# A two-layer decoder on one core: another order of the layers, and one more set of narrow heads under way

## The chip, the core and the metric

The kernel runs on one NeuronCore of a Trainium2 chip. Its engines work side by side, each through a queue of its own: TensorE (PE in the profile, PEld for its weight loads) multiplies, VectorE (DVE) and ScalarE (ACT) work element by element, GpSimd (POOL) does the same more slowly, and SyncE (SP) issues transfers between the device's memory (HBM) and the on-chip memory (SBUF). Matrix products land in PSUM[...]. The metric is the device time of one execution in microseconds; lower is better.

## What is computed

`x` is 16 sequences of 128 positions of 256 numbers. Six layers follow one another, each as `x = layernorm(x + f(x))`:

```
0  wide attention   16 heads of 64, causal: softmax(q k' / 8) v, then W_O
1  ensemble         8 experts, each relu(x P_in') P_out', weighted by a gate per token
                    gate[b,s,e] = sum_k ctx[b,k,s] * (itok[b,k,s] == e)
2  routed           2 shared experts + 16 routed ones, top 2 of a softmax over 16 logits;
                    every expert computed, h = silu(x wg) * (x wu) * comb
3  narrow attention 16 heads of 16, band of +-8 positions
4  cross attention  16 heads of 16, keys and values from ctx
5  dense experts    8 experts of gelu(x w1 + b1) w2 + b2, summed, one scale per token
```

All of it is in float32. No sequence looks at another one, so the 16 sequences are independent; within a sequence each layer needs the one before.

## The kernel before

**Tiling.** The sequences are cut into four groups of four (`GB = 4`, `T = 512` tokens). A group's activations stay on chip as `x` (tokens on partitions) and, rebuilt after each layer by `tail`, as the transposed `xT`. A pair (layer, group), such as (3, 2), is the unit of work in what follows.

**Pieces and streams.** Each layer is a Python generator. It issues a handful of instructions and then yields an estimate of their TensorE time in microseconds, or `UNTIL` with a moment before which the next piece had better not be issued. A `Weaver` decides whose piece comes next. It keeps a clock `now`, which is the sum of the yielded estimates, and it takes a piece from a *main* stream and a *side* stream by their shares: each piece adds its estimate, divided by that stream's figure in the pair `us`, to the stream's share, and the stream with the smaller share goes next among those whose `UNTIL` has come. Short streams (the transposes, routing and gates of `tail`) go ahead of both. The engines then run their queues in the order so woven, moved about a little by the framework's scheduler; nothing of the weaving exists at run time. All real waiting is by semaphores, and PSUM and SBUF buffers come from small rotating pools.

**Main and side.** The attentions (layers 0, 3 and 4) are the main stream, one group after another. The dense layers (1, 2 and 5) are the side stream `dense`, one chain (lines 880 to 883). A layer of a group may begin when the tail of the layer before has been issued (`run`, line 847):

```python
        yield lambda: written[g] == number - 1
```

Before, the main stream's (0, 0) goes alone, then seven stretches each weave one group's attention with the side chain, and the rest of `dense` goes alone at the end.

**Layer 1 to layer 2.** After (1, g) its tail transposes `x`, then `route` (lines 670 to 726) makes 16 small matmuls (L675), some twenty short DVE instructions in a chain (softmax, best of 16 twice, weights, ending in `r_o`, L715), a transpose of `r_o` on TensorE (line 720) and a transfer to HBM. Only then may (2, g) begin, with the matmuls that read `ws`.

**Dense layers.** `accumulate` (line 578) keeps one chunk ahead: it issues the products `psH` of chunk i + 1 (L289), whose result ACT (Gelu, L813, layer 5) or DVE (L650, layer 1) turns into `hT`, and then the eight passes `psM` of chunk i that read `hT` (L589).

**Wide attention**, `attention0` (line 343): 16 units of two pairs of heads and one sequence. Each goes through scores `psS` (L384), softmax, transposes of the weights `e` (L51), weighing with `v` (L426) and output (L393).

**Narrow attention**, `attention16` (line 447), serves layers 3 and 4: 8 units of one sequence and half of the heads. A unit's scores take two matmuls of 64 rows (L464, halves k = 0 and k = 1) into the only `psS` buffer. `softmax` (line 306) takes a minimum with the mask (layer 3 alone), row maxima on DVE, eight Exp instructions with their sums on ACT (L325), reciprocals on DVE and the scaling of `e` on POOL (L331). Then come eight transposes of `e` on TensorE (L51), two copies to `eT` on ACT (L340), eight passes with `v` (L476), and `hz` and `zT`. The loop of lines 500 to 522 is a software pipeline: in round n it issues the scores of unit n, the transposes of unit n - 1, the output of n - 3 and the weighing of n - 2. It holds the transposes back by 14 us of the weaver's clock after the scores. The pool of `e` has three buffers, that of `eT` four (two for each unit).

Of the kernel before, what the change touches and what calls it, by code (L numbers as in the profile page):

```python
# [27 lines left out]
def kernel(ctx: ExitStack, tc: tile.TileContext, a: dict, out: bass.AP):  # L28
# [15 lines left out]
    def bank(tag):  # L44
        return ps.tile([P, T], F32, tag=tag, name=f"ps{tag}")
# [7 lines left out]
    def together(first, *steps):  # L53

        for step in steps:
            tc.add_manual_dep(
                first.ins, step.ins.name,
                mybir.DependencyInfo(mybir.DependencyClass.Sync, mybir.DependencyReason.DATA),
                reason="together",
            )  # L60
# [172 lines left out]
    weaver = Weaver()  # L233
# [72 lines left out]
    def softmax(s, seen):  # L306

        n = 2 * s.shape[2]
        if seen is not None:
            sm = p2.tile([P, n, P], F32, tag="s", name="sm")  # L310
            nc.vector.tensor_tensor(
                sm.rearrange("p (s h) k -> p s h k", s=2), s,
                seen.unsqueeze(1).unsqueeze(1).to_broadcast([P, 2, n // 2, P]), ALU.min,
            )
        nmax = sp.tile([P, n], F32, tag="nmax", name="nmax")
        if seen is not None:
            nc.vector.tensor_reduce(nmax, sm, AX.X, ALU.max, negate=True)  # L317
        else:
            nc.vector.tensor_reduce(  # L319
                nmax.rearrange("p (s h) -> p s h", s=2), s, AX.X, ALU.max, negate=True  # L320
            )
        e = p3.tile([P, n, P], F32, tag="p", name="e")
        total = sp.tile([P, n], F32, tag="total", name="total")
        for h in range(n):
            nc.scalar.activation(  # L325
                e[:, h, :], sm[:, h, :] if seen is not None else s[:, h // (n // 2), h % (n // 2), :],
                AF.Exp, bias=nmax[:, h:h + 1], accum_out=total[:, h:h + 1],
            )
        inv = sp.tile([P, n], F32, tag="inv", name="inv")
        nc.vector.reciprocal(inv, total)  # L330
        nc.gpsimd.tensor_tensor(e, e, inv.unsqueeze(2).to_broadcast([P, n, P]), ALU.mult)  # L331
        return e

    def weights_T(e):

        pt = bank("O").rearrange("p (h q) -> p h q", h=4)
        for h in range(4):
            transpose(pt[:, h, :], e[:, h, :])
        eT = p4.tile([P, 4, P], F32, tag="pt", name="eT")
        return eT, nc.scalar.copy(eT, pt)  # L340
# [106 lines left out]
    def attention16(x, qT, kT, v, wo, bo, seen):  # L447
        norm = Norm(x)
        norm.bias(bo)

        def scores(b, c):

            at = slice(b * P, (b + 1) * P)

            kb = p2.tile([P, 4, P], F32, tag="kb", name="kb")
            nc.gpsimd.tensor_tensor(  # L456
                kb, kT[:, c, at].unsqueeze(1).to_broadcast([P, 4, P]),
                hm4.unsqueeze(2).to_broadcast([P, 4, P]), ALU.mult,
            )
            yield UNTIL, weaver.now + 2.0  # L460
            s = ps.tile([P, 2, T], F32, tag="S", name="psS", bufs=1)
            for k in range(2):
                rows = slice(64 * k, 64 * k + 64)
                mm(  # L464
                    s[:, k, :], lhsT=qT[rows, c, at], rhs=kb[rows].rearrange("p h k -> p (h k)"),
                    start=True, stop=True,
                )
            return softmax(s.rearrange("p s (h k) -> p s h k", h=4), seen)

        def weigh(b, c, eT):  # L470


            pz = bank("O")[:, :D].rearrange("p (k q) -> p k q", k=2)
            for r in range(4):
                rows = slice(32 * r, 32 * r + 32)
                step = mm(  # L476
                    pz[rows], lhsT=v[:, b, c * P + 32 * r:c * P + 32 * r + 32],
                    rhs=eT[r // 2][0][:, 2 * (r % 2):2 * (r % 2) + 2, :],
                    start=True, stop=True,
                )  # L480
                if r == 0:
                    together(step, eT[1][1])
            if c == 0:
                zT[b] = p3.tile([P, 2, P], F32, tag="z", name="zT16")
            half_z = p2.tile([P, P], F32, tag="hz", name="hz")
            nc.scalar.activation(half_z, pz[:, 0, :], AF.Copy, scale=even[:, 0:1])
            nc.vector.scalar_tensor_tensor(
                out=zT[b][:, c, :], in0=pz[:, 1, :], scalar=even[:, 1:2], in1=half_z,
                op0=ALU.mult, op1=ALU.add,
            )  # L490

        def output(b):
            po = bank("H")[:, :D]
            for k in range(KC):
                mm(po, lhsT=zT[b][:, k, :], rhs=wo[:, k, :], start=k == 0, stop=k == KC - 1)  # L495
            norm.add(b, po)

        units = [(b, c) for b in range(GB) for c in range(2)]
        e, eT, zT, at = {}, {}, {}, {}
        for n in range(len(units) + 4):  # L500
            if n < 8:
                e[n] = yield from scores(*units[n])
                at["e", n] = weaver.now + 14.0
                yield 1.06
            m = n - 1
            if m in e:
                yield UNTIL, at["e", m]
                got = e.pop(m)
                eT[m] = [weights_T(got[:, 4 * k:4 * k + 4, :]) for k in range(2)]
                at["t", m] = weaver.now + 3.5  # L510
                yield 1.0
            m = n - 3
            if ("z", m) in at and units[m][1] == 1:
                yield UNTIL, at["z", m]
                output(units[m][0])
                yield 0.86
            m = n - 2
            if m in eT:
                yield UNTIL, at["t", m]
                weigh(*units[m], eT.pop(m))  # L520
                at["z", m] = weaver.now + 3.0
                yield 0.63
        norm.done()
# [321 lines left out]
    def run(number, g):  # L845

        yield lambda: written[g] == number - 1
        x, xT = xs[g], xTs[g]
        if number == 0:
            yield from attention0(x, xT, g)  # L850
        elif number == 1:
            yield from ensemble0(x, xT, g)
        elif number == 2:
            yield from experts0(x, xT, extra[g])
        elif number == 3:
            yield from attention1(x, xT)
        elif number == 4:
            yield from cross1(x, xT, g)
        else:
            yield from experts1(x, xT, extra[g])  # L860
            nc.sync.dma_start(
                out=out[g * GB:(g + 1) * GB].rearrange("b p d -> p b d"), in_=x
            )
            return
        weaver.short.append(Stream(tail(number, g)))

    def chain(*layers):
        for layer in layers:
            yield from run(*layer)

    def sum_biases():
        pb = bank("H")[:, :D]
        mm(pb, lhsT=ones[0:8, :], rhs=b2, start=True, stop=True)
        nc.vector.tensor_copy(b2sum, pb)
        yield 0.5
# [2 lines left out]
    b2sum = cp.tile([P, D], F32, tag="b2sum", name="b2sum")  # L878
    weaver.short += [Stream(tail(-1, g)) for g in range(NG)]
    dense = Stream(chain(  # L880
        (1, 0), (2, 0), (1, 1), (2, 1), (1, 2), (2, 2), (1, 3), (2, 3),
        (5, 0), (5, 1), (5, 2), (5, 3),
    ))
    weaver.weave(Stream(chain((0, 0))))
    weaver.short.append(Stream(sum_biases()))
    weaver.weave(Stream(chain((0, 1))), dense, (81.0, 110.0))
    weaver.weave(Stream(chain((0, 2))), dense, (81.0, 106.0))
    weaver.weave(Stream(chain((0, 3))), dense, (81.0, 106.0))
    weaver.weave(Stream(chain((3, 0), (4, 0))), dense, (68.0, 110.0))
    weaver.weave(Stream(chain((3, 1), (4, 1))), dense, (68.0, 106.0))  # L890
    weaver.weave(Stream(chain((3, 2), (4, 2))), dense, (68.0, 106.0))
    weaver.weave(Stream(chain((3, 3), (4, 3))), dense, (68.0, 110.0))
    weaver.weave(dense)


# [67 lines left out]
```

## Time and profile before

| | |
|---|---|
| median of the runs | 1867.82 us (1865.88 to 1871.24, three runs) |
| the profiled execution | 1863.81 us, its span 1862.1 us |
| matmul instructions on TensorE | 7794, busy 1805.6 us, 97% of the span |
| ScalarE | busy 750.1 us, 40% |
| VectorE | busy 648.7 us, 35% |
| GpSimd | busy 363.0 us, 19% |
| HBM traffic | 129.04 MB read, 71 GB/s over the span |

A float32 matmul appears as two passes in the trace and a transpose as one. Passes overlap in the pipeline, so a pass of 128x512 lasts about 0.6 us in the table of groups, while the next one starts 0.43 us after it; sums of TensorE work are made with such start-to-start times. The windows further down give the busy time of each engine in a stretch, the granted TensorE clock (PEclk) and the traffic.

### The profile page before, as it was taken

The numbers are of one execution on the slowest core, as the hardware profiler recorded it, in microseconds if no ns is written. First come the engines' busy times: TensorE is split into PE (matmuls) and PEld (weight loads), VectorE is DVE, ScalarE is ACT, GpSimd is POOL, SyncE is SP. The second block draws the span as 40 slices with busy tenths as digits, with TensorE's granted clock in tenths as the row PEclk, the third lists the DMA queues.
The fourth block names the chain that finished last, engine by engine and source line by source line (L and its number), as shares of the span: only waits on it lengthen the run. The fifth ranks groups of instructions, "written<-read, shape, count | busy, mean of one in ns | idle before, by whom it ended". The sixth has DMA issues, their size and how long they took to land.

```text
span 1862.1 us, 21229 instructions
## 1 busy us (share of the span) xinstructions
PE 1805.6 (97%) x7794; PEld 1111.5 (60%) x7794; DVE 648.7 (35%) x1359; ACT 750.1 (40%) x2229; POOL 363.0 (19%) x297
## 2 busy tenths in 40 slices
PE   6999999999999999999899999899999999999998
PEld 3656666566666656656455665465565655556665
DVE  3453334434333525343425444333223222312101
ACT  2541222342312333241452423527748468475221
POOL 4210001121101112122332213223122122221000
PEclk9999999999999999999899999999999999999999
DMA  6021123122221132122123121121111111111220
GB/s 233 24 86 57 57 74 102 58 85 74 99 89 37 44 120 101 63 71 66 41 79 108 63 91 34 58 93 66 46 63 57 46 68 46 57 46 68 80 76 26
DMA packets 67272, 132.72 MB, mean 71 GB/s; under 512 B 6600, under 2 KB 34304, under 8 KB 67168
## 3 DMA queue, kind: packets, MB, share of 16 engines
q1 hardware_dynamic: 66240, 129.20, 20.5%
q0 software_dynamic: 928, 2.17, 0.4%
q8 instruction: 62, 1.02, 0.2%
q14 instruction: 42, 0.34, 0.1%
HBM read 129.04 MB, written 2.29 MB: 71 GB/s over the span
## 4 chain that ended last, share of the span: by engine, by line
PE 81%; issue 7%; ACT 5%; DVE 5%; DMA 1%; POOL 1%; SPq 0%; POOLq 0%; DVEq 0%; ACTq 0%
PE psH L289 34%; PE psM L589 23%; PE psH L298 4%; PE psO L51 4%; PE psS L464 3%; PE psH L393 3%; ACT e L325 2%; PE psS L384 2%; PE psO L426 2%; PE psO L476 2%; PE psH L495 1%; PE psH L51 1%; DMA wquad<-in_L_attn_W_Q 1%; ACT L325 1%; DVE x L281 1%
## 5 line engine op out<-in xcount | busy, mean ns | idle before, releaser
L589 PE MATMUL psM<-we,hT 128*128 128x256 f32 x2048 | 496.2, 383 | 3.1 <-ACT hT L813 3.1
L289 PE MATMUL psH<-xT,we 128*128 128x512 f32 x1024 | 488.3, 598 | 1.3 <-DVE hT L650 1.3
L589 PEld LDWEIGHTS psM<-we,hT 128*128 128x128 f32 x2048 | 380.7, 190 | 153.1 <-issue 95.1
L331 POOL TENSOR_TENSOR e<-e,inv 128x512 f32<-128x512 f32 (+1 forms) x128 | 188.2, 1471 | 792.6 <-DVE inv L330 728.2
L289 PEld LDWEIGHTS psH<-xT,we 128*128 128x128 f32 x1024 | 187.4, 190 | 159.9 <-issue 142.0
L325 ACT ACTIVATE e<-sm,nmax 128x128 f32<-128x128 f32 x512 | 198.5, 389 | 152.9 <-DVE nmax L317 152.5
L340 ACT COPY eT<-psO 128x512 f32<-128x512 f32 x192 | 106.0, 586 | 207.2 <-PE psO L51 206.7
L650 DVE SCALAR_TENSOR_TENSOR hT<-psH,gt 128x512 f32<-128x512 f32 x128 | 88.1, 689 | 214.1 <-PE psH L289 214.1
L813 ACT ACTIVATE hT<-psH,b 128x512 f32<-128x512 f32 x128 | 86.9, 687 | 177.1 <-PE psH L289 176.5
L289 PE MATMUL psH<-xT,wquad 128*128 128x512 f32 x256 | 117.7, 603 | 1.3 <-DVE qT L357 0.8
L51 PEld LDWEIGHTS psO<-ident,e 128*128 128x128 f32 x768 | 88.4, 143 | 49.4 <-issue 32.1
L51 PE MATMUL psO<-ident,e 128*128 128x128 f32 x768 | 111.0, 281 | 5.0 <-POOL e L331 4.9
L289 PE MATMUL psH<-xT,wr 128*128 128x512 f32 x256 | 115.8, 594 | 0.0
L456 POOL TENSOR_TENSOR kb<-kT,hm 128x512 f32<-128x512 f32 x64 | 66.9, 1046 | 189.4 <-PE psS L464 128.7
L330 DVE RECIPROCAL inv<-total 128x4 f32<-128x4 f32 (+1 forms) x128 | 23.9, 187 | 216.6 <-ACT e L325 214.0
L325 ACT ACTIVATE e<-psS,nmax 128x128 f32<-128x128 f32 x256 | 90.1, 379 | 21.3 <-DVE nmax L319 20.9
L325 ACT ACTIVATION_READ_ACCUMULATOR e<-sm,nmax 128x1 f32 x512 | 95.8, 187 | 0.0
L464 PE MATMUL psS<-kb,qT 64*128 64x512 f32 x256 | 84.5, 646 | 7.0 <-ACT e L325 6.7
L279 POOL TENSOR_TENSOR rstd<-ve,mhalf 128x4 f32<-128x4 f32 x24 | 24.3, 1012 | 310.0 <-DVE ve L277 309.4
L317 DVE TENSOR_REDUCE nmax<-sm 128x4 f32<-128x512 f32 (+1 forms) x96 | 82.8, 863 | 2.7
L289 PEld LDWEIGHTS psH<-xT,wquad 128*128 128x128 f32 x256 | 47.2, 191 | 58.3 <-issue 50.2
L289 PEld LDWEIGHTS psH<-xT,wr 128*128 128x128 f32 x256 | 48.0, 190 | 49.5 <-issue 46.3
(155 smaller groups left out, 1802.9 us busy)
## 6 DMA issues: line engine op xcount, KB each, us to landing
we<-in_L_ffn_w SPq DMA_DIRECT2D x64, 512.0 KB
we<-in_L_xattn_proj_in SPq DMA_DIRECT2D x32, 512.0 KB
we<-in_L_xattn_proj_out SPq DMA_DIRECT2D x32, 512.0 KB
gt<-gatesd SPq DMA_DIRECT2D x32, 256.0 KB
cw<-combd SPq DMA_DIRECT2D x64, 128.0 KB
wquad<-in_L_attn_W_Q SPq DMA_DIRECT2D x16, 256.0 KB
wquad<-in_L_attn_W_K SPq DMA_DIRECT2D x16, 256.0 KB
wquad<-in_L_attn_W_V SPq DMA_DIRECT2D x16, 256.0 KB
```

The source lines that it names most:

```text
L51: return nc.tensor.transpose(out_, in_, ident[:n, :n])
L289: mm(pt, lhsT=w[:, c, cols], rhs=xT[:, c, :], start=c == 0, stop=c == KC - 1)
L298: mm(pv[:, i, :], lhsT=xT[:, c, (b + i) * P:(b + i + 1) * P], rhs=w[:, c, :], start=c == 0, stop=c == k - 1,)
L317: nc.vector.tensor_reduce(nmax, sm, AX.X, ALU.max, negate=True)
L325: nc.scalar.activation(e[:, h, :], sm[:, h, :] if seen is not None else s[:, h // (n // 2), h % (n // 2), :], AF.Exp, bias=nmax[:, h:h + 1 ...
L331: nc.gpsimd.tensor_tensor(e, e, inv.unsqueeze(2).to_broadcast([P, n, P]), ALU.mult)
L340: return eT, nc.scalar.copy(eT, pt)
L456: nc.gpsimd.tensor_tensor(kb, kT[:, c, at].unsqueeze(1).to_broadcast([P, 4, P]), hm4.unsqueeze(2).to_broadcast([P, 4, P]), ALU.mult,)
L464: mm(s[:, k, :], lhsT=qT[rows, c, at], rhs=kb[rows].rearrange("p h k -> p (h k)"), start=True, stop=True,)
L589: step = mm(acc[b], lhsT=held[:, b * P:(b + 1) * P], rhs=down(i), start=i == 0 and b % 2 == 0, stop=i == n - 1, skip_group_check=True,)
L650: nc.vector.scalar_tensor_tensor(out=hT, in0=ph, scalar=0.0, in1=gates[e], op0=ALU.max, op1=ALU.mult)
L813: nc.scalar.activation(hT, ph, AF.Gelu, bias=b1[:, i:i + 1])
```

## The change

Two things are altered. The pipeline of `attention16` gets one more stage between the scores of a unit and its transposes: in round n it now transposes unit n - 2, weighs n - 3 and outputs n - 4, and the hold-back is 16 us instead of 14. And the two streams are ordered anew: the first two wide attentions go alone; the side chain takes layer 1 of two groups, then layer 2 of the same two groups; the main stream runs in three stretches of two groups each. The figures that set the shares change from 81 : 110 or 81 : 106 to 81 : 150, and from 68 : 110 or 68 : 106 to 68 : 150 for the narrow layers.

```diff
-        for n in range(len(units) + 4):
+        for n in range(len(units) + 5):
             if n < 8:
                 e[n] = yield from scores(*units[n])
-                at["e", n] = weaver.now + 14.0
+                at["e", n] = weaver.now + 16.0
                 yield 1.06
-            m = n - 1
+            m = n - 2
             if m in e:
...
-            m = n - 3
+            m = n - 4
             if ("z", m) in at and units[m][1] == 1:
...
-            m = n - 2
+            m = n - 3
             if m in eT:
...
-        (1, 0), (2, 0), (1, 1), (2, 1), (1, 2), (2, 2), (1, 3), (2, 3),
+        (1, 0), (1, 1), (2, 0), (2, 1), (1, 2), (1, 3), (2, 2), (2, 3),
         (5, 0), (5, 1), (5, 2), (5, 3),
     ))
-    weaver.weave(Stream(chain((0, 0))))
+    weaver.weave(Stream(chain((0, 0), (0, 1))))
     weaver.short.append(Stream(sum_biases()))
-    weaver.weave(Stream(chain((0, 1))), dense, (81.0, 110.0))
-    weaver.weave(Stream(chain((0, 2))), dense, (81.0, 106.0))
-    weaver.weave(Stream(chain((0, 3))), dense, (81.0, 106.0))
-    weaver.weave(Stream(chain((3, 0), (4, 0))), dense, (68.0, 110.0))
-    weaver.weave(Stream(chain((3, 1), (4, 1))), dense, (68.0, 106.0))
-    weaver.weave(Stream(chain((3, 2), (4, 2))), dense, (68.0, 106.0))
-    weaver.weave(Stream(chain((3, 3), (4, 3))), dense, (68.0, 110.0))
+    weaver.weave(Stream(chain((0, 2), (0, 3))), dense, (81.0, 150.0))
+    weaver.weave(Stream(chain((3, 0), (4, 0), (3, 1), (4, 1))), dense, (68.0, 150.0))
+    weaver.weave(Stream(chain((3, 2), (4, 2), (3, 3), (4, 3))), dense, (68.0, 150.0))
     weaver.weave(dense)
```

No instruction of the arithmetic is added or taken away, and none changes its shape. The built program holds the same 4393 matmuls and the same 420 transfers on SyncE, in another order; of the loads of ACT's function tables, which are placed where the order of functions asks for one, there are 102 where there were 109.

## The prediction, made before the change was run

> **What bounds the kernel now.** I read the page first, then windows cut where TensorE's idle time changes character, then the order of time in the worst of them.
>
> ```profile
> PE 1805.6 (97%) x7794; PEld 1111.5 (60%) x7794; DVE 648.7 (35%) x1359; ACT 750.1 (40%) x2229; POOL 363.0 (19%) x297
> PEclk9999999999999999999899999999999999999999
> PE 81%; issue 7%; ACT 5%; DVE 5%; DMA 1%; POOL 1%; SPq 0%; POOLq 0%; DVEq 0%; ACTq 0%
> ```
>
> TensorE is busy 97% of the span. The matmuls stay the same, so only TensorE's waits, its slow clock and the seams between its instructions can change. The windows say where those lie (busy time and instructions by engine, clock, DMA):
>
> ```profile
> 24.00:125.00 101.00, 96.77 (x533) 59.34 (x532) 52.72 (x100) 46.26 (x170) 23.22 (x20) 1.00 0.23 79
> 125.00:896.00 771.00, 767.45 (x3427) 481.85 (x3425) 307.26 (x622) 230.24 (x753) 117.54 (x98) 1.00 0.22 74
> 896.00:922.00 26.00, 18.37 (x87) 9.31 (x88) 14.01 (x40) 14.69 (x61) 9.08 (x7) 0.80 0.12 33
> 922.00:1150.00 228.00, 226.53 (x932) 135.40 (x931) 87.53 (x168) 82.09 (x292) 57.93 (x41) 1.00 0.23 75
> 1150.00:1180.00 30.00, 23.03 (x111) 12.77 (x109) 20.12 (x57) 15.71 (x62) 11.79 (x8) 0.89 0.09 28
> 1180.00:1660.00 480.00, 471.66 (x1941) 280.15 (x1940) 137.70 (x287) 292.50 (x750) 115.30 (x81) 1.00 0.18 62
> ```
>
> Two short windows, 896 to 922 and 1150 to 1180, are bad: TensorE idles 7.6 and 7.0 us and its clock falls to 0.80 and 0.89. The timeline of TensorE in the first (start, us, instructions, idle before):
>
> ```profile
> 907.30 1.30 PE L464 MATMUL psS<-kb,qT 64*128 64x512 f32 x4 [2.65 <-ACT e L325]
> 909.51 1.97 PE L51 MATMUL psO<-ident,e 128*128 128x128 f32 x8 [0.91 <-POOL e L331]
> 911.41 1.08 PE L476 MATMUL psO<-eT,v 128*32 128x256 f32 x8
> 914.63 1.02 PE L51 MATMUL psH<-ident,r_o 128*16 128x128 f32 x4 [2.14 <-DVE r_o L715]
> 915.45 5.05 PE L289 MATMUL psH<-xT,ws 128*128 128x512 f32 x8
> ```
>
> This is the passage from (1,2) to (2,2). The side stream has only `route` until r_o is transposed, so cross attention alone feeds TensorE, and its softmax cannot keep up. The other window is (1,3) to (2,3).
>
> [...] after the waits above the first eight `ws` passes took 4.98 us (915.45 to 920.43) against 8 x 0.43 = 3.44. [...] when the two halves of L464 stand together: 1.06 us for both (770.80 to 771.86); apart, one half alone took 1.05 (1258.41 to 1259.46). [...] the trace has the 1283 ns, but the next ACTIVATE starts about 0.02 us later, so I price 1.3 us.
>
> **The change part by part**, against the profiled execution (1863.8 us; its span is 1862.1, and 1.7 lie around it).
>
> *Layer 1 of two groups, then layer 2 of both.* While (1,0) is being routed, (1,1) now runs; while (1,1) is routed, (2,0). Both bad windows lose their cause. Their price: the passes in 896 to 922 at undisturbed start-to-start times (0.43 for 512 columns, 0.216 for 256, 0.109 for 128, 0.11 for L675, 1.06 for a pair of L464) come to 13.4 us, so 12.6 of 26 are lost, clock included. In 1150 to 1180 the same count gives 19.1, so 10.9 are lost. Together -23.5. What is late next is `route` itself: between its matmuls and the transpose of r_o the order held 5.7 and 5.9 us of TensorE work in the bad cases and 11.6 and 11.0 in the two good ones, where almost no wait shows. The changed order holds 11.3, 9.6, 11.6 and 13.2. The 9.6 may cost 1: +1.
>
> *Split pairs.* Of the 64 narrow units, the halves of L464 stand apart in 10 before and in 6 after (order of TensorE's instructions). Each costs 1.05 more: -4. Other changes of tile shape cost 0.09 each and move both ways (1296 runs of equal instructions become 1324); I take 0, between -2 and +2.
>
> *(0,1) alone.* The first attention alone runs from about 24 to 122 and ends badly:
>
> ```profile
> PE psH L393 <- ACT zT L432: 1.7, 5, 0.5
> PE psH L298 <- DVE qT L357: 1.4, 1, 1.4
> PE psH L289 <- DVE qT L357: 0.8, 1, 0.8
> ```
>
> TensorE is idle 4.2 us in the window 24 to 125. (0,1) now has the same order without a filler, its last four softmaxes again with only 4.1 to 5.1 us of TensorE work between scores and transposes; it loses the cover it had, and (0,0)'s gates come on DVE during it (eight instructions of about 0.7 us, beside DVE at 52%). I take +4, from +2 to +12. The same work leaves the woven part, and more dense work ends up alone after the last attention, where the trace shows no waits: 0.
>
> *Narrow heads two deep.* The transposes mostly get 13 to 19 us of TensorE work after the scores; before, eight of the 64 units had under 9. This removes the remaining waits of psO on POOL (2.3 us from 1180 to 1660). It is free in buffers: three `e` and four `eT` are just enough. But the holding back no longer paces the units. Between the first and last scores of (3,2), (4,2), (3,3), (4,3) the order held 55, 59, 56 and 57 us of TensorE work; now 41, 48, 42 and 48. The units come closer, and projections lie apart from them. ACT has to follow, while layer 5 gives it Gelus:
>
> ```profile
> L813 ACT ACTIVATE hT<-psH,b 128x512 f32<-128x512 f32 x78 | 52.7, 687 | 62.3 <-PE psH L289 61.7
> L325 ACT ACT_TABLE_LOAD x34 | 43.6, 1283 | 15.4 <-DVE nmax L319 11.2 <-DVE nmax L317 3.3
> L813 ACT ACT_TABLE_LOAD x33 | 42.3, 1283 | 2.8 <-PE psH L289 2.2
> ```
>
> (groups on ACT from 1180 to 1660: busy, mean ns). A unit there costs ACT eight Exps (3.1, start to start), two table loads (2.6), two eT copies (0.95), hz (0.3) and one or two Gelus of 0.6: about 7.9 us. At the new distances (41/7 to 48/7, 5.9 to 6.9 us) ACT cannot keep that up; before it had about 8. Seven distances in four stretches are short by some 1 to 2 us each, 40 us in sum; but each stretch begins and ends with slack, the units may lag by a round (their waits allow 13 to 19 us where 8 to 9 are needed), and 14 us remain as overflow when ACT's work is summed in slices of 20 us. Who waits is not the softmax but the Gelu behind it in ACT's queue, and L589 behind that. Before, those waits were 3.1 us. I take +8, from 0 to +20.
>
> *Transfers.* The same 420 on SP, each moved with its stream. Two wide attentions alone draw 1 MB each 20 us, about 50 GB/s, where the first slice of the page moved 233; dense weights come as before, into three buffers. Routing's transfer now stands long before the loads of layer 2, so SP is held there less. TensorE waited for weights once from 125 to 700 (0.4 us). 0.
>
> Sum: -23.5 + 1 - 4 + 4 + 8, and -2 for the waits of psO = -16.5, so 1847 for an execution like the profiled one. The median of the runs shown is 4 us above that execution; I put the forecast at **1850**, some 1% faster.
>
> **The rivals.** (a) *ACT takes most of it back*: the overflow is paid in full and the split of units and projections adds as much again, +20 instead of +8, and the lone attention costs 8: 1866 on the median's footing at worst, 1862 as its middle. For it: ACT 61% busy from 1180 to 1660 and denser stretches. Against: before, with single slices just as full, the waits named were small. (b) *The waits go and nothing comes*: 0 for ACT, +2 for (0,1): 1839. For it: the slack of the softmax. Against: the sums above. (c) *Slower*: in the denser stretches nearly every Gelu lands behind a block of Exps. Place: L589 <- ACT hT L813, during layer 5. Price: the block with its table is 4.5 us (1305.48 to 1309.96 in the trace), plus 1.3 and 0.7: 6.5 us from psH to hT, where the order gives 4.5 to 7.4. The 62 table loads left there make 31 such Gelus; at 1.3 us each, 40 us instead of 8, giving 1882. It decides from about 0.9 us each (28 us, which eats the gain). Against: 33 such switches before cost 3.1 us. (d) *The windows move*: cross attention starves elsewhere, as at (3,0) or behind the longer lone start; 1867. Against: the side stream is never without work in the new order once it has begun.
>
> **How the numbers follow.** Forecast 0.55 (1842 to 1857), (a) 0.17, (b) 0.10, (c) 0.11, (d) 0.07. About 0.3% (5.6 us) is what a measurement of this kernel can tell from no change, so faster means below 1862.2: forecast, (b) and half of (a), with a little of (d): 0.75. Within: 0.13, from (a) and (d). Slower: (c) and a little of (a): 0.12. The range for 8 in 10 is 1836 to 1868; it takes in (b), (a) and (d), and leaves out (c).
>
> **What would show it.** Right: no window of 30 us with a clock below 0.95 after the start; `route`'s wait for r_o under 1 us a time; L464's waits for `e` and L51's for POOL nearly gone; a stretch at 24 to 210 with some 8 us of idle TensorE; L589's waits for hT somewhat above 3.1. Wrong: L589 <- ACT hT of 20 us and more, or psS <- ACT e grown in (4,2) and (4,3); or waits of TensorE on a DMA of weights near 200, where the side stream starts later.

## The result, and the profile after

The changed kernel takes 1851.81 us (median of four runs, 1850.99 to 1852.02); the kernel before, run beside it, took 1869.53 (1865.88 to 1871.46). The ratio is 0.9907, with a 95% interval of 0.9889 to 0.9925: faster by 0.9%. The profiled execution took 1850.99 us against 1863.81, its span 1849.3 against 1862.1.

The same lines of the page as before, for the changed kernel:

```profile
PE 1799.3 (97%) x7794; PEld 1109.2 (60%) x7794; DVE 648.2 (35%) x1359; ACT 737.7 (40%) x2222; POOL 362.2 (20%) x297
PEclk9999999999999999999999999999999999999999
PE 80%; issue 7%; ACT 6%; DVE 4%; DMA 1%; POOL 1%; SPq 0%; POOLq 0%; ACTq 0%; DVEq 0%
```

The 8 in the row of clocks is gone, and TensorE is as full as before. Where time was lost is read from windows. First the kernel before, in windows that suit both kernels (busy time and instructions by engine, clock, DMA share, GB/s):

```profile
150.00:250.00 100.00, 99.59 (x436) 63.87 (x435) 32.00 (x55) 22.16 (x82) 8.32 (x8) 1.00 0.22 74
700.00:950.00 250.00, 241.13 (x1034) 144.32 (x1034) 107.21 (x215) 96.63 (x338) 62.81 (x45) 0.98 0.21 69
950.00:1150.00 200.00, 198.74 (x826) 119.86 (x823) 80.24 (x156) 66.46 (x247) 49.78 (x36) 1.00 0.23 76
```

Then the changed kernel:

```profile
24.00:150.00 126.00, 121.89 (x666) 74.31 (x664) 70.40 (x129) 59.43 (x218) 26.32 (x23) 1.00 0.21 68
150.00:250.00 100.00, 96.19 (x518) 59.89 (x517) 46.39 (x92) 35.81 (x127) 13.48 (x13) 1.00 0.19 59
700.00:950.00 250.00, 249.16 (x1063) 149.21 (x1062) 110.12 (x228) 83.20 (x326) 62.88 (x45) 1.00 0.25 83
950.00:1150.00 200.00, 196.16 (x815) 115.94 (x814) 84.35 (x167) 90.44 (x306) 56.14 (x40) 0.99 0.21 64
```

From 700 to 950, where the first bad window lay, TensorE's idle time fell from 8.9 to 0.8 us. From 150 to 250 it rose from 0.4 to 3.8: there the second wide attention now drains without a filler. And from 950 to 1150 it rose from 1.3 to 3.8, of which 2.95 lie in one place. TensorE around it, in order of time (start, us, instructions, idle before):

```profile
1085.00 1.13 PE L464 MATMUL psS<-kb,qT 64*128 64x512 f32 x4
1086.06 3.70 PE L289 MATMUL psH<-xT,ws 128*128 128x512 f32 x8
1092.71 2.08 PE L464 MATMUL psS<-kb,qT 64*128 64x512 f32 x4 [2.95 <-issue]
1094.71 1.22 PE L589 MATMUL psM<-ws,hT 128*128 128x256 f32 x2
```

Scores of one unit start at 1085.00, and those of the next stand only eight passes behind. They write the same PSUM tile, of which there is one. ACT in the same stretch:

```profile
1088.41 1.28 ACT L325 ACT_TABLE_LOAD   x1 [4.43 <-DVE nmax L319]
1089.71 0.37 ACT L325 ACTIVATE e<-psS,nmax 128x128 f32<-128x128 f32 x1
...
1092.12 0.40 ACT L325 ACTIVATE e<-psS,nmax 128x128 f32<-128x128 f32 x1
```

The eighth Exp that reads the tile starts at 1092.12 and ends at 1092.52, and the next scores follow at 1092.71. The profile names no releaser ("issue"); that the scores waited for the tile is read from these times. The row maxima had waited behind a normalization and a product on DVE (1.38 us from 1085.22, 0.68 from 1086.52), and a table load of 1.28 us came on top. During the wait TensorE's clock fell to half, for 3.4 us from 1092.4 (0.57 was granted from 1092 to 1096): the pair of halves took 2.00 us instead of 1.06.

To add such losses up I used one measure for all kernels. For each run of equal instructions in TensorE's order, its undisturbed time (from start-to-start times in the trace of the kernel before) is subtracted from its time in the trace. What remains is lost time: waits and slow clock. What is taken as undisturbed is a choice, and other choices move the differences between kernels by a few microseconds, so small terms of these sums are uncertain. In microseconds, from TensorE's first pass to its last:

| | before | after |
|---|---|---|
| undisturbed work | 1759.9 | 1753.8 |
| lost, start to 40 us | 17.0 | 16.0 |
| lost, 40 to 250 (lone wide attentions) | 8.8 | 14.9 |
| lost, 250 to 700 | 9.6 | 8.8 |
| lost, 700 to 1180 (both bad windows) | 33.5 | 15.4 |
| lost, 1180 to the end (layer 5 with narrow heads) | 19.1 | 26.2 |
| sum | 1848.0 | 1835.2 |

The windows gave back 18.1, the undisturbed work 6.1, the start and the stretch from 250 to 700 together 1.8; the lone attention took 6.1 and the stretch of layer 5 took 7.1. That is the -12.8 of the two spans. The medians differ by 17.7; the kernel before was seen between 1862 and 1874 us in later runs, with medians of 1865.5 to 1866.5, which puts the change at 14 to 15 us there.

### The profile page after: what moved, and what is told of

It is laid out like the page before. It is cut to its first block, busy times and chain, and to the rows that moved or that the text cites. A ratio compares the mean times of both kernels' runs of the same rounds, so it can differ in the third digit from the quotient of the medians.

```text
span 1849.3 us, 21302 instructions
## 1 busy us (share of the span) xinstructions
PE 1799.3 (97%) x7794; PEld 1109.2 (60%) x7794; DVE 648.2 (35%) x1359; ACT 737.7 (40%) x2222; POOL 362.2 (20%) x297
## 4 chain that ended last, share of the span: by engine, by line
PE 80%; issue 7%; ACT 6%; DVE 4%; DMA 1%; POOL 1%; SPq 0%; POOLq 0%; ACTq 0%; DVEq 0%
PE psH L289 33%; PE psM L589 24%; PE psH L298 4%; PE psO L51 4%; PE psS L464 3%; ACT e L325 3%; PE psH L393 3%; PE psO L476 2%; PE psS L384 2%; PE psO L426 2%; PE psH L495 1%; PE psH L51 1%; ACT L325 1%; DMA wquad<-in_L_attn_W_Q 1%; DVE x L281 1%
## 5 line engine op out<-in xcount | busy, mean ns | idle before, releaser
L589 PE MATMUL psM<-we,hT 128*128 128x256 f32 x2048 | 498.7, 384 | 4.1 <-ACT hT L813 4.1
L589 PEld LDWEIGHTS psM<-we,hT 128*128 128x128 f32 x2048 | 381.8, 191 | 144.2 <-issue 92.9
L813 ACT ACTIVATE hT<-psH,b 128x512 f32<-128x512 f32 x128 | 87.1, 687 | 227.7 <-PE psH L289 227.4
L464 PE MATMUL psS<-kb,qT 64*128 64x512 f32 x256 | 79.9, 648 | 6.2 <-issue 3.8
```

Of the source, the lines that this page charges most:

```text
L464: mm(s[:, k, :], lhsT=qT[rows, c, at], rhs=kb[rows].rearrange("p h k -> p (h k)"), start=True, stop=True,)
L589: step = mm(acc[b], lhsT=held[:, b * P:(b + 1) * P], rhs=down(i), start=i == 0 and b % 2 == 0, stop=i == n - 1, skip_group_check=True,)
L813: nc.scalar.activation(hT, ph, AF.Gelu, bias=b1[:, i:i + 1])
```

## Experiments

Each kernel ran in turn with the kernel before on the same chip; times are medians, and ratios are to the kernel before with their 95% intervals. "Lost" is the measure above.

### 1. One pair swapped in the side chain, nothing else

```diff
-        (1, 0), (2, 0), (1, 1), (2, 1), (1, 2), (2, 2), (1, 3), (2, 3),
+        (1, 0), (2, 0), (1, 1), (2, 1), (1, 2), (1, 3), (2, 2), (2, 3),
```

> The kernel before with one edit: the side chain's third and fourth layer-1 and layer-2 pairs stand as (1,2), (1,3), (2,2), (2,3). Theory (the two windows without a filler are the gain): both windows of before go, -23.5, and split pairs of scores fall from 10 to 6, -4, so about 1868 - 25 = 1843 us or a little more, since no pipeline of the heads and no lone attention is touched; no window after the start with a TensorE clock below 0.95. Rival (the starved stretch only moves): 1862 to 1868, with a new window of low clock elsewhere.

1847.91 us, ratio 0.9897 (0.9878 to 0.9915). Lost time from 700 to 1180 fell from 33.5 to 9.6, by 23.9. Windows of this kernel:

```profile
700.00:950.00 250.00, 249.11 (x1086) 151.82 (x1086) 110.65 (x224) 87.22 (x327) 59.54 (x42) 1.00 0.24 79
1150.00:1250.00 100.00, 97.79 (x416) 58.68 (x414) 32.27 (x81) 51.46 (x134) 31.41 (x22) 1.00 0.23 76
```

No window is idle or slow where the two bad ones stood, and the clock stays whole until the tail of the kernel (0.998 over the whole span, against 0.994 before). So the missing filler during routing was the cause of both, and this one line alone is worth as much as the whole change. The time is 5 us above the theory's, since from 1180 on 29.0 us are lost instead of 19.1. The wait that grew most there, in TensorE's waits from 1180 to 1700 (us in total, times, longest), first in the kernel before, then in this one:

```profile
PE psM L589 <- ACT hT L813: 3.1, 6, 0.9
```

```profile
PE psM L589 <- ACT hT L813: 9.2, 11, 2.7
```

### 2. The new order with the old pipeline of the heads

The changed kernel, with lines 498 to 523 as they were before.

> The changed kernel with the narrow heads' pipeline as before (transposes of unit n - 1, hold-back 14). Theory: the order of layers carries the gain; -23.5 for the windows, +4 to +5 for the second lone attention, nothing for split pairs (10 as before), and none of the 8 to 9 us that denser units cost ACT: 1849 to 1853, the same as the changed kernel. Rival (the deeper pipeline of the heads carries the gain): above 1860.

1864.44 us, ratio 0.9988 (0.9981 to 0.9995): almost nothing gained, and my theory missed by at least 11 us. The windows did go (lost from 700 to 1180: 17.7), and the lone attention cost what it costs in the changed kernel (14.8 from 40 to 250). But from 1180 on 29.5 us are lost, 10 more than before, although the units are spaced as before; and the undisturbed work is 1759.3, nothing below before, with 10 split pairs. So the deeper pipeline is worth 12.6 us in this order. By the traces the two kernels lie 13.5 apart: 5.5 of undisturbed work, 3.3 of lost time after 1180, 2.3 between 700 and 1180, and 2.3 at the start, which has nothing to do with it. This order also loses 8 us more from 700 to 1180 than that of experiment 1, and it has the second lone attention, which that one has not. The figures of the shares (150 instead of 106 or 110) changed with the order, and no run changes them alone, so what they do stays open.

### 3. The new pipeline of the heads with the old order

```diff
-                at["e", n] = weaver.now + 14.0
+                at["e", n] = weaver.now + 16.0
...
-            m = n - 1
+            m = n - 2
```

and likewise for the stages behind.

> The kernel before with the narrow heads' pipeline alone changed (transposes of unit n - 2, hold-back 16). Theory: in the order of TensorE the work between the routing matmuls and the transpose of r_o is 4.8 us in the third passage and 9.0 in the fourth (4.3 and 4.2 before), so one window stays (12 us) and the other shrinks (-8 or so); split pairs 5 instead of 10, -5; denser units cost ACT +8: about 1868 - 5 = 1863, from 1855 to 1868. Rival (the heads carry the gain): 1852 or less.

1874.79 us, ratio 1.0041 (1.0029 to 1.0053): slower by 8 us, where I had expected a small gain. Two windows of this kernel:

```profile
700.00:950.00 250.00, 240.89 (x1050) 144.11 (x1050) 110.70 (x223) 95.25 (x354) 62.20 (x44) 0.95 0.19 64
1150.00:1250.00 100.00, 87.79 (x345) 50.96 (x343) 48.66 (x109) 39.05 (x128) 25.08 (x19) 0.90 0.17 51
```

TensorE is idle for 9.1 and 12.2 us, and the clock is lower than before (0.98 and 0.97 there). In the clock's records it stands at half for 23.9 us from 907.9, and for 17.1 and 3.4 us from 1194.7 and 1218.6; before, for 10.2 and 6.8 us. I had counted work between the routing matmuls and r_o alone, and left out the other waits of a starved stretch: around the first spell TensorE waits 3.8 us for `e` before scores, 1.8 for r_o and 1.8 for `x`. The likely reason, which no run takes apart, is that with the side stream empty TensorE lives on the narrow units, and a deeper pipeline does not make their softmax faster. In the spells of 23.9 and 17.1 us TensorE was busy 18.7 and 13.2 us at half speed.

### 4. The changed kernel, (0,1) woven again

```diff
-    weaver.weave(Stream(chain((0, 0), (0, 1))))
+    weaver.weave(Stream(chain((0, 0))))
     weaver.short.append(Stream(sum_biases()))
-    weaver.weave(Stream(chain((0, 2), (0, 3))), dense, (81.0, 150.0))
+    weaver.weave(Stream(chain((0, 1))), dense, (81.0, 110.0))
+    weaver.weave(Stream(chain((0, 2), (0, 3))), dense, (81.0, 106.0))
```

> The changed kernel with (0,1) woven with the side chain again (81 : 110, then (0,2) and (0,3) at 81 : 106). Theory: the lone (0,1) cost 4 to 6 us, which comes back, while the order of instructions has one more split pair (+1): 1846 to 1849. Rival (a second lone attention costs nothing, its stalls are structural): 1852 or a little more.

1845.68 us, ratio 0.988 (0.9859 to 0.99): the lowest median of the kernels that compute the whole function, 6.1 below the changed kernel's, though run in another set, and with ratios whose intervals overlap. Lost time from 40 to 250 falls from 14.9 to 8.7. TensorE's waits from 24 to 250 in the changed kernel:

```profile
PE psH L393 <- ACT zT L432: 3.3, 10, 0.5
PE psH L289 <- DVE qT L357: 2.0, 2, 1.2
```

and in this one:

```profile
PE psH L393 <- ACT zT L432: 1.7, 5, 0.5
PE psH L298 <- DVE qT L357: 1.0, 1, 1.0
```

Each attention that ends alone has its five waits of L393, 1.7 us in all; these are a part of the 6.2 alone. TensorE's idle time elsewhere moves both ways: from 250 to 700 it rises from 1.8 to 3.1, and from 700 to 1180 it falls from 5.1 to 1.9. So that the whole gain equals the loss of the lone attention is in part chance. By the lost time, the second attention alone is a loss in this kernel, not a gain.

### 5 and 6. Layer 5 without its own function table

```diff
-            nc.scalar.activation(hT, ph, AF.Gelu, bias=b1[:, i:i + 1])
+            nc.scalar.activation(hT, ph, AF.Identity, bias=b1[:, i:i + 1])
```

once in the changed kernel and once in the kernel before. Both leave out layer 5's nonlinearity, so they compute another function.

> The changed kernel with Identity in place of Gelu in layer 5 (so layer 5's nonlinearity is left out), which needs no table of its own: 41 table loads instead of 102, some 79 us of ACT less, the queue orders otherwise nearly the same (split pairs 4 instead of 6, about -2). Theory (ACT, with its table loads, makes the waits of the woven stretches of layer 5): the waits of L589 for hT and what goes with them after 1150 us fall by 12 to 20 us: 1832 to 1839 us. Rival (the waits there come from the distances between units, from DVE and POOL): 1848 to 1852, by the split pairs alone.

> The kernel before with Identity in place of Gelu in layer 5 (layer 5's nonlinearity is left out): 35 table loads instead of 109, split pairs 5 instead of 10 (-5). Theory: the same effect as in the changed kernel but smaller, since before some 20 us of waits stood after 1050 us outside the windows and 35 in the changed kernel: -5 for split pairs and -5 to -8 for waits, 1853 to 1857; the windows stay, though the second, where layer 5 has not begun, keeps its 11 us. Rival: 1861, by the split pairs alone.

1835.09 us from the changed kernel (ratio 0.9832, 0.9815 to 0.9849), 1849.9 from the kernel before (0.9911, 0.9892 to 0.993). The first is 16.7 below the changed kernel, as the theory had it; the second is 15.6 below the kernel before, 3 to 7 more than it had. Lost time after 1180 falls from 26.2 to 11.2, and from 19.1 to 9.1. The window from 1200 to 1700 in the changed kernel, and then with Identity:

```profile
1200.00:1700.00 500.00, 487.89 (x2024) 294.47 (x2023) 139.22 (x292) 297.20 (x787) 116.08 (x81) 0.99 0.17 57
```

```profile
1200.00:1700.00 500.00, 497.46 (x2080) 302.61 (x2079) 139.41 (x295) 221.29 (x730) 117.24 (x82) 1.00 0.17 59
```

ACT's busy time falls by 76 us and TensorE's idle time from 12.1 to 2.5 (in the kernel before, from 8.3 to 0.0). Neither kernel has a wait of L589 for hT left in its list of waits there. So ACT with its switching between Exp and Gelu makes most of what is lost in this stretch: 15 of 26 us in the changed kernel, 10 of 19 before. Of the 7.1 us by which the change makes it worse, 5 go with the table loads. The change itself is worth the same with Identity (14.8 us) as with Gelu.

### 7. The swap of experiment 1 with the deeper pipeline

> The kernel before with both: the side chain's (1,2), (1,3), (2,2), (2,3) as in the first experiment, and the narrow heads' pipeline of the changed kernel. Theory (the deeper pipeline gains where the side stream always has work and loses where it has none, since then the units' own distances feed TensorE): 6 to 9 us faster than the swap alone (one split pair less, fewer changes of shape, fewer waits of transposes for their e), 1839 to 1842. Rival (it loses 8 us everywhere, as it did alone on the kernel before): 1855.

1851.53 us, ratio 0.9918 (0.9901 to 0.9936): 3.6 above the swap alone, so the theory misses, and the rival too, which had it lose 8. Lost time from 700 to 1180 is 22.1 where the swap alone had 9.6; with a new wait of 1.8 us before L464 at 910 the clock stands at half for 6.8 us. After 1180 it falls from 29.0 to 24.9, and the undisturbed work by 2.5. The pipeline cost 8.3 and 3.6 us in two orders and saved 12.6 in a third; its worth depends on the order around it.

### 8. Experiment 4 with a hold-back of 14 us

```diff
-                at["e", n] = weaver.now + 16.0
+                at["e", n] = weaver.now + 14.0
```

> The changed kernel with (0,1) woven again, as in the fourth experiment, and the narrow heads' hold-back at 14 us instead of 16. Split pairs 3 instead of 7 (-4); 116 table loads instead of 117. Theory (the hold-back beyond what the softmax needs is worth nothing by itself): the split pairs alone, 1840 to 1843. Rival (less hold-back brings the waits for e back): 1848 or more.

1849.68 us, ratio 0.9917 (0.9893 to 0.9941), 4 above experiment 4, with intervals that overlap. The undisturbed work is 5.8 lower, as counted, and lost time from 700 to 1180 is 9.5 higher. TensorE's waits before L464 for `e` come to 4.5 us from 700 to 1180 and 2.7 from 1180 to 1700, where experiment 4 has none. By these numbers the rival is right.

### 9 to 12. Both halves of the scores held together

```diff
-                mm(
+                step = mm(
                     s[:, k, :], lhsT=qT[rows, c, at], rhs=kb[rows].rearrange("p h k -> p (h k)"),
                     start=True, stop=True,
                 )
+                tc.keep_in_program_order(step)
```

in the kernel before, the changed kernel, experiment 4's and experiment 1's.

> The kernel before, with both halves of a narrow unit's scores held in program order, so that they stand together: 0 split pairs instead of 10. Theory (a split pair costs 1.05 us, and the halves of the seams in the two windows are hidden by the waits there): 6 of the ten stand outside the windows, so -6 to -10: 1856 to 1860. Rival (a split costs nothing[...]): 1864 to 1867.

> The changed kernel with both halves of the scores held together: 0 split pairs instead of 6. Theory: -6, so 1845 to 1847. The difference from the ninth experiment is then the change without its effect on split pairs, 10 to 13 us. Rival: 1851 to 1852.

> The fourth experiment's kernel ((0,1) woven) with both halves of the scores held together: 2 split pairs instead of 7. Theory: -5, so 1840 to 1842, the fastest of all if the parts add. Rival: 1846, no gain, because holding the order moves other instructions.

> The first experiment's kernel (one pair of groups swapped in the side chain) with both halves of the scores held together: 1 split pair instead of 6. Theory: -5, so 1842 to 1844. Rival: 1848.

| kernel | us | without this edit | undisturbed work | lost after 1180 |
|---|---|---|---|---|
| before | 1866.76 (1.0002, 0.999 to 1.0014) | 1866.19 | 1759.9 to 1748.5 | 19.1 to 31.2 |
| changed | 1856.83 (0.9951, 0.9933 to 0.9969) | 1851.81 | 1753.8 to 1748.4 | 26.2 to 33.2 |
| (0,1) woven | 1846.53 (0.9897, 0.9875 to 0.9919) | 1845.68 | 1756.3 to 1751.6 | 24.6 to 32.0 |
| one pair swapped | 1860.46 (0.9966, 0.9957 to 0.9975) | 1847.91 | 1756.9 to 1752.6 | 29.0 to 42.0 |

No kernel gained, against the theory in all four. The undisturbed work fell by 11.4, 5.4, 4.7 and 4.3 us, close to 1.05 us for each of the 10, 6, 5 and 5 pairs joined; and after 1180 as much or more is lost again. (In the changed kernel and in experiment 1's, TensorE also idles 3.4 and 3.2 us longer from 950 to 1150.) With all pairs joined, the change is worth 9.9 us, where 10 to 13 were expected. The waits that take most of it, from 1180 to 1700 in the kernel before with joined pairs (the edit moves L589 and L813 down by a line):

```profile
PE psM L590 <- ACT hT L814: 9.0, 8, 4.5
PE psO L51 <- POOL e L331: 5.1, 4, 1.5
```

and in experiment 12:

```profile
PE psM L590 <- ACT hT L814: 17.4, 12, 2.7
```

The waits for hT were 3.1 in the kernel before and 9.2 in experiment 1. Their growth, 3.7 to 8.2 us in the four kernels, is about half to two thirds of what is lost again after 1180. The longest of them shows how it happens. TensorE in the kernel before, and then with joined pairs:

```profile
1430.94 1.13 PE L464 MATMUL psS<-kb,qT 64*128 64x512 f32 x4 [2.54 <-ACT e L325]
1432.94 1.35 PE L589 MATMUL psM<-we,hT 128*128 128x256 f32 x5 [0.87 <-ACT hT L813]
```

```profile
1432.14 2.07 PE L590 MATMUL psM<-we,hT 128*128 128x256 f32 x4 [4.54 <-ACT hT L814]
```

ACT does the same in both there: a table load, eight Exps, another load and the Gelu, only some 0.8 us earlier with joined pairs. Before, the scores stood in the middle of this wait and took 1.06 us of it; with joined pairs they stand elsewhere, and TensorE waits as much longer. So here a saving of TensorE's time turns into waiting for ACT. Whether this holds for all of it is not shown: holding the order also moved 22 to 41 of the 2120 other instructions on ACT, though it left no more table loads (103 for 109, 100 for 102, 113 for 117, 111 for 119).

## Why the prediction was right, and where it was not

The forecast was 1850 us against 1851.81, and the cause of the gain was the one named. That the number came so close is in part luck. The steps added up to -16.5 us for one profiled execution against another, and these lie 12.8 apart. The forecast came nearer because it was put 3 us up, for a median that stood 4 us above the profiled execution before; after the change the median stood only 0.8 above it. By its steps:

- **Both windows, -23.5.** Right in place and size: experiment 1 alone gave back 23.9 us from 700 to 1180. In the changed kernel only 18.1 of them show, because a new wait took the place of some: the scores at 1092.71, behind the one PSUM tile. The prediction counted the `route` chain as what is late next (+1) and did not count the distance between scores: eight passes, 3.4 us of TensorE work, stood between two of them in (4,1), and the Exps of the first ended 7.5 us after its scores began. `route` itself leaves no wait for r_o among TensorE's waits.
- **Split pairs, -4.** Right as a term of TensorE's work: 1.05 us each, and -6.1 in all with the seams that were put at 0. Wrong as a gain in time: experiments 9 to 12 removed 4 to 11 us of such work without any gain. Most of the pairs stand after 1180, where much of the saving was waited for again behind ACT. The 6.1 saved and part of the 7.1 lost after 1180 may thus be one effect; the runs do not separate them.
- **(0,1) alone, +4.** Measured +6.1 in lost time, inside its bounds of 2 to 12. The median of experiment 4 is also 6.1 us lower, where other stretches moved too.
- **Narrow heads two deep, +8 for ACT.** The size was right, 7.1 us, and so was ACT for most of it: 5 of the 7.1 go with the table loads (experiments 5 and 6). The step that failed is its cause, "But the holding back no longer paces the units". Experiments 1 and 2 keep the old pipeline and its spacing and lose 10 us more than before in the same stretch; the changed kernel loses less than they do. The list of distances was also short in one place: it left out the time that a split unit spans, and from the first scores to the last of (3,3) the changed order holds 69 us where it held 65. Only three of the four stretches became denser. Why ACT's waits grow when the windows go, even at the old spacing, was not settled: ACT is no busier there (312.6 us from 1200 to 1700 in experiment 1, 315.1 before), so it may be a matter of when its work comes.
- **The waits for e on POOL, -2.** 4.9 to 2.1 us over the span. For POOL's speed beside DVE's, in the kernel before: a product over 128x512 took 1.27 us on POOL (L756) and 0.69 on DVE (L745).
- **Transfers, 0.** TensorE waited once for a wide attention's weights, 1.0 us against 0.4.

Of the signs named, that of the clock failed narrowly: 3.4 us at half from 1092.4 make about 0.94 of a window of 30 us. L464's waits for `e` did not nearly go (2.4 us, and 3.8 under "issue"). The other signs came: TensorE idles 6.6 us from 24 to 210 (some 8 were named) and 7.9 up to 250, the waits for r_o are gone, and L589 waits 4.1 us for hT.

In the kernel before, the clock's records show half speed for 10.2 us from 908.1, so the passes after 915.45 began in it; the longest single wait of that stretch was 2.65 us. In the changed kernel waits of 2.95 us (before 1092.71), 2.14 us (before 1467.59) and 2.41 us (before 1609.84) each came with 3.4 us at half speed. The length of a wait alone does not tell, for in experiment 5 the same scores wait as long and run at full speed behind it:

```profile
1095.33 1.13 PE L464 MATMUL psS<-kb,qT 64*128 64x512 f32 x4 [2.95 <-issue]
```

Experiment 1 has a wait of 3.1 us before L476 that costs no clock (1.00 was granted from 1200 to 1700), while experiment 12 has one of the same length at the same instruction with 3.4 us at half speed (0.99). In the kernel before, a wait of 3.10 us (before 1176.21) costs none either: the eight `ws` passes behind it took 3.5 us. So a wait of 2.1 us came with a slow clock, and one of 3.1 us did not; how long a wait has to be for it is not shown.

On the loads of ACT's function tables: they took 1283 ns each in the traces of both kernels, and behind the one at 1088.41 the next ACTIVATE started 0.02 us after its end (1089.71). The price of 1.3 us for a switch agrees with experiment 6: from 1180 to 1700 it has 7 loads where the kernel before has 79, which makes 92.4 us less of loads, and ACT's busy time there fell by 90.0 us, from 323.7 to 233.7.

## What to carry to other kernels

When two streams share an engine, look first for the stretches where one of them has only a short, serial chain to do, and give the other stream's next independent unit to it. That exchange for one pair of groups, alone, gave as much here as the whole change (experiment 1), while the whole new order without the deeper pipeline gave almost nothing (experiment 2); an order has to be tried with what runs beside it. Before you count matmul time saved as time gained, ask which engine ends the waits in that very stretch: TensorE was 97% busy over the span, and yet the 4 to 11 us of its work that experiments 9 to 12 saved brought no time, and about half to two thirds of what was lost again during layer 5 were waits for ACT.

## What the runs showed that was not expected

The value of a deeper software pipeline depended on the order around it: it cost 8.3 and 3.6 us in two orders and saved 12.6 in a third. And TensorE's clock fell to half around single waits of 1.8 us (experiment 7, for 6.8 us) to 3.1 us (experiment 12, for 3.4 us), while a wait of 2.95 us in experiment 5 left it whole, where the same wait in the changed kernel cost 3.4 us at half; in the kernel with the deeper pipeline alone, where waits follow close upon one another, a spell lasted 23.9 us.
